# Output operands of an adaptive-layernorm block prepared in two steps, the layernorm written in place, the output pools laid out in another order, and the slices of down weights taken earlier

## The chip, the cores and the metric

The kernel runs on one core of a Trainium2 chip. The metric is the device time of one execution in microseconds (us); lower is better. Differences of less than about 0.3% can't be told from no change.

## The reference

Everything is float32. There are two sequences (b = 0, 1) of 1024 tokens of 1024 features. A vector per sequence gives six modulation vectors (shift, scale and gate for the attention and for the feed-forward part).

```python
mod = (_silu(L0_c) @ L0_wmod).reshape(L0_c.shape[0], 6, 1, -1)
...
h = _layernorm(x, axis=-1) * (1 + ca) + sa
x = x + ga * _L0_attn_ref(h, ...)     # 32 heads of 32, q/k layernorm, ALiBi, causal softmax, output projection
h = _layernorm(x, axis=-1) * (1 + cb) + sb
x = x + gb * _L0_ffn_ref(h, ...)      # out = (silu(gate) * up) @ Wd.T * ad, inner width 2752
```

## The kernel before

All large products are done by a Strassen-like scheme with seven products of half-size blocks (`seven`, names P1, P2, U2, P5, U3, P53, U6 in this order), which needs sums of blocks of both operands (S1 to S4 of the left one, T1 to T4 of the weights). The kernel has these stages:

1. Projections to q, k and v of sequence 0, then of sequence 1 (`projections`), in pairs of token tiles: a pair j is 256 tokens, four pairs per sequence and per part q, k, v. In the loop over the pairs of sequence 1 the function `side` is called after each of the seven products. It advances `down_weights`, which forms the sums T1 to T4 of the feed-forward part's down weights in 20 slices: each slice loads four blocks of 128 KB, subtracts four times on GpSimd (lines 1215 to 1218) and stores four blocks (line 1221), in three steps, 60 steps in all. In the kernel before, the first step comes at call 24 of 84.
2. Attention (`attention`), in units of one group of four heads and one block of keys: scores on TensorE, exponentials on ScalarE (line 1085), masks on GpSimd (line 1089), the product with v on TensorE, and sums of the probabilities on VectorE and GpSimd (line 1117). At the end of a group `settle` adds up the sums with a product with ones, and for the last group of 512 queries `reciprocals` marks these queries as settled.
3. Output projection, residual and second layernorm (`output`), pair by pair: four pairs of sequence 0, then two of sequence 1 beside the attention of sequence 1, then the last two of sequence 1 beside other feed-forward rows (`rest_rows`).
4. The feed-forward part: gate and up products, then down products.

`together` interleaves stage 2 with stages 1 and 3: it takes units of attention and pieces of dense work by a share of their planned times, so TensorE's instructions follow an order written at build time, in which they are pinned. The order of the other engines' instructions, and of the loads and stores that SyncE issues, is made by the framework's scheduler, which simulates the program and takes whatever is ready by its own estimate, earlier program lines first. It is therefore not the program order, but it is fixed at build time, and each engine then works through its own list in order.

What one output pair does: `operand` makes the left operand. It loads the reciprocals of the softmax sums (rb, four loads, line 1249) and four blocks of the attention's output (aoA: A11, A12, A22, A21, line 1263), multiplies each block by the reciprocals (line 1264, two on VectorE and two on GpSimd), and forms S1, S2 on VectorE and S3, S4 on GpSimd (lines 1265 to 1269; S3 overwrites A21). Of its tiles only A21 has two buffers; rb, A11, A12, A22, S1, S2, S4 have one. `output` then loads the residual (xr, two tiles of 128 x 1024, line 1292), runs the seven products, and `read` evacuates each: P1, U2 and P5 are copied by ScalarE (line 1299), the others are added on VectorE (1307, or 1305 for U6), multiplied by the gate ga and added to xr on GpSimd (1308, 1309). The sum xr is stored to x1 (line 1314) and normalized into a second tile xn (`normalize`: statistics at 729 and 730, reciprocal root at 734 to 745, the result at 747). In the pair after, xn is transposed by TensorE in four pieces through the one shared bank, which VectorE empties into h2t (line 869); h2t is stored for the feed-forward part (lines 1200, 1329). The shared bank also serves `settle` (the matmul with ones, emptied at 1127).

Memory: pools are stacked in the order in which they are opened, and a pool's first use waits until every earlier pool that it overlaps has been released. The output stage's pools (hb, wo, oga, tok, opart, osmall, ao, restw) take the place of the projections' pools (a, w, raw, part, qs, xin, qsmall) and of the slices' pool (wdsum) above them. The first pair's operand is made ahead of the output weights (wB_o and wT_o, lines 824 and 828). restw holds the last columns of the gate and up weights (line 1374, 1.5 MB).

Of the kernel before, what the change touches and what calls it, by code (L numbers as in the profile page):

```python
# [12 lines left out]
FP = mybir.dt.float32  # L13
# [5 lines left out]
P = 128  # L19
# [461 lines left out]
def kernel(  # L481
# [20 lines left out]
    B, S, D = x.shape  # L502
# [6 lines left out]
    QB = 512  # L509
# [41 lines left out]
    NJ = NT // 2  # L551
# [111 lines left out]
    with tc.tile_pool(name="prep", bufs=1) as prep, tc.tile_pool(  # L663
        name="wmod", bufs=2 * KC
# [176 lines left out]
    def seven(a, bt, banks, read, between, grain):  # L841

        x, y = banks.pair()
        for c_, qa, qb_, q in SEVEN:
            bank = x if c_ == "x" else y
            first = q in ("P1", "P2", "P5")
            for j in range(KC // 2):
                matmul(
                    bank, a(qa, j), bt[qb_][:, j, :],
                    start=(first and j == 0), stop=(j == KC // 2 - 1), skip_group_check=True,  # L850
                )
                if j % grain == grain - 1 and j < KC // 2 - 1:
                    banks.made += 1
                    yield grain * MM
                    yield from between(q)
            read(q, bank)
            banks.made += 1
            yield grain * MM
            yield from between(q)
# [154 lines left out]
    settled = set()  # L1014
# [169 lines left out]
    def alone(dense):  # L1184
        for _ in dense:
            pass
# [56 lines left out]

    def operand(b, j, ap_, own=None):

        qb, y0 = 2 * j * P // QB, 2 * j * P % QB
        rb = ap_.tile([P, KC, 2 * P], FP, tag="rb", name=f"rb_{b}_{j}")
        for g in range(4):
            nc.sync.dma_start(
                rb[ts(g, HD)],  # L1250
                rec_dram[b][qb].rearrange("(k g) q -> g k q", g=4)[g][:, ds(y0, 2 * P)].partition_broadcast(HD),
            )
        a = {
            q: (ap_ if q == "S4" or own is None else own).tile(
                [P, KC // 2, P], FP, tag=q, name=f"ao{q}_{b}_{j}",
                bufs=2 if q == "A21" and own is None else None,
            )
            for q in ("A11", "A12", "A21", "A22", "S1", "S2", "S4")
        }
        for m, kh, q, eng in (  # L1260
            (0, 0, "A11", nc.vector), (0, 1, "A12", nc.gpsimd), (1, 1, "A22", nc.vector), (1, 0, "A21", nc.gpsimd),
        ):
            nc.sync.dma_start(a[q], ao_dram[b][qb][:, ds(kh * 4, 4), ds(y0 + m * P, P)])
            eng.tensor_mul(a[q], a[q], rb[:, ds(kh * 4, 4), ts(m, P)])
        nc.vector.tensor_add(a["S1"], a["A21"], a["A22"])
        nc.vector.tensor_sub(a["S2"], a["S1"], a["A11"])  # L1266
        a["S3"] = a["A21"]
        nc.gpsimd.tensor_sub(a["S3"], a["A11"], a["A21"])
        nc.gpsimd.tensor_sub(a["S4"], a["A12"], a["S2"])
        return a  # L1270

    gates = {}

    def output(b, js, pools, banks, bt, todo, keep, made={}, q0=1):

        gap_, ap_, tkp, partp, hbp, sm = pools
        while (b, 2 * js[0] * P // QB) not in settled:
            yield None
        if b not in gates:
            gates[b] = gap_.tile([P, D], FP, tag="ga", name=f"ga_{b}")  # L1280
            nc.sync.dma_start(gates[b], gate_dram[2][b].partition_broadcast(P))
        ga = gates[b]

        for j in js:
            while (b, 2 * j * P // QB) not in settled:
                yield None
            qts = (2 * j, 2 * j + 1)
            a = made.get((b, j)) or operand(b, j, ap_)
            xs = []
            for m in range(2):  # L1290
                xr = tkp.tile([P, D], FP, tag="xr", name=f"xr_{b}_{qts[m]}")
                nc.sync.dma_start(xr, x[b, ts(qts[m], P), :])
                xs.append(xr)
            part_t = {}

            def read(q, bank):
                if q in ("P1", "U2", "P5"):
                    part_t[q] = partp.tile([P, 512], FP, tag=q, name=f"o{q}_{b}_{j}")
                    nc.scalar.copy(part_t[q], bank)
                    return  # L1300
                m, n = QUAD[q]

                yg = part_t[MATE.get(q, "P5")]
                if q == "U6":
                    nc.vector.tensor_mul(yg, ga[:, ts(n, HALF)], bank)
                else:
                    nc.vector.tensor_add(yg, yg, bank)
                    nc.gpsimd.tensor_mul(yg, yg, ga[:, ts(n, HALF)])
                nc.gpsimd.tensor_add(xs[m][:, ts(n, HALF)], xs[m][:, ts(n, HALF)], yg)

            yield from seven(lambda q, i: a[q][:, i, :], bt, banks, read, todo.places(q0, 1), 2)
            yield from todo.run(len(todo.list), True)
            for m in range(2):
                nc.sync.dma_start(x1_dram[b * NT + qts[m]], xs[m])
            xn = []
            for m in range(2):
                t_ = tkp.tile([P, D], FP, tag="xn", name=f"xn_{b}_{qts[m]}", bufs=2)
                xn.append(t_)
            todo.first(normalize(xs, xn, sm, f"f{b}_{j}"), b == 1 and j >= NJ // 2 - 1)
            h2 = keep(b, j)  # L1320
            for m in range(2):
                for g in range(2):
                    def go(bank, m=m, g=g, xn=xn, h2=h2, j=j):
                        turned(
                            xn[m], bank, lambda k: h2[:, k, m, :],
                            lambda k: modt[:, 4, k, b : b + 1], lambda k: modt[:, 3, k, b : b + 1], g, False,
                        )
                        if (m, g) == (1, 1):
                            nc.sync.dma_start(h2_dram[b][j], h2)
                            if b == 0:  # L1330
                                inner_b("B11", h2[:, 0 : KC // 2], j, hbp, nc.vector)
                                inner_b("B21", h2[:, KC // 2 :], j, hbp, nc.vector)
                    todo.add(go)
# [21 lines left out]
    OUT_US = 112.0  # L1355
# [70 lines left out]
    with ExitStack() as st:  # L1426
# [9 lines left out]
        banks = Banks(three[0:2], three[2:3] + more[2:5])  # L1436
# [52 lines left out]
    ost = ctx.enter_context(ExitStack())  # L1489
# [8 lines left out]
    out_args = []  # L1498

    def dense_work():  # L1500
        yield from dense0
        with tc.tile_pool(name="wdsum", bufs=2) as dwp:
            steps = itertools.chain.from_iterable(down_weights(i, dwp) for i in range(4 * NSB))

            def side(n, e):

                if 7 * n + e >= 24:
                    next(steps, None)

            yield from projections(1, qpools, banks, 1, side=side)  # L1510
            for _ in steps:
                pass
        early.close()
        hbp = right["hb"] = ost.enter_context(tc.tile_pool(name="hb", bufs=1))
        wop = ost.enter_context(tc.tile_pool(name="wo", bufs=1))
        gap_, tkp, partp, osm, aop = [
            ost.enter_context(tc.tile_pool(name=n, bufs=k))
            for n, k in (("oga", 1), ("tok", 3), ("opart", 1), ("osmall", 1), ("ao", 1))
        ]
        opools = (gap_, aop, tkp, partp, hbp, osm)  # L1520
        made = {(0, 0): operand(0, 0, opools[1])}
        bt = weights_b(wop, wout_t, "o", wt_dram[3])
        rwp = ost.enter_context(tc.tile_pool(name="restw", bufs=1))
        out_args.extend((opools, banks, bt, Todo(banks), keep))
        yield from output(0, range(NJ), *out_args, made)
        right["w"] = rest_weights(rwp, nc.sync)
        yield from output(1, range(NJ // 2), *out_args)

# [13 lines left out]
    opools, _, bt, todo, _ = out_args  # L1542
# [3 lines left out]
    wide = rest_st.enter_context(tc.tile_pool(name="wide", bufs=1, side="right"))  # L1546
# [20 lines left out]
    fetch(0, 0, nc.scalar)  # L1567
    rest_w = right["w"]
    fetch(1, 0, nc.scalar)
    made = {(1, NJ // 2): operand(1, NJ // 2, opools[1], wide)}  # L1570
    made[1, NJ // 2 + 1] = operand(1, NJ // 2 + 1, opools[1])
    fetch(0, 1)
    with_turns(rows((0, 0), (1, 0)))
    fetch(1, 1)
# [1 line left out]
    def between():  # L1576
        yield from rows((0, 1))
        second(0)
        yield from rows((1, 1))

    together(
        between(), output(1, range(NJ // 2, NJ), *out_args, made, 3), lambda a: 0.6 * OUT_US / 2 * a / 20.6
    )
    in_range(rest_pool, rps)
    fetch(0, 2)
# [53 lines left out]
    with ExitStack() as ff:  # L1639
# [9 lines left out]
        with ExitStack() as gu:  # L1649
# [83 lines left out]
            for s in range(NSB):  # L1733
# [66 lines left out]
                for n_, (oa, ob, frm, to) in enumerate(STAGES):  # L1800
# [18 lines left out]
                    for e, (c_, qa, qb_, q) in enumerate(CHAIN):  # L1819
                        bt = bts[e] if e < len(bts) else moving(s, n_, e)  # L1820
                        for mat in ("g", "u"):
# [7 lines left out]
                            f_, t_ = tiles[mat]  # L1829
# [222 lines left out]
```

## Time and profile before

| quantity | value |
|---|---|
| median of three timed runs | 2902.21 us (2901.19 to 2909.03) |
| profiled execution: its time, its span | 2896.01 us, 2894.3 us |
| TensorE matmul busy | 2702.2 us (93%) |
| VectorE, ScalarE, GpSimd busy | 1453.0, 685.2, 1296.8 us |
| moved by DMA | 579.14 MB, mean 200 GB/s |
| HBM read, written | 411.89 MB, 165.17 MB |
| first and last matmul with output weights | 916.0, 1495.6 us |

Times within the kernel count from the start of the profiled span. PE is TensorE, PEld its weight loads, DVE VectorE, ACT ScalarE, POOL GpSimd, and SPq SyncE's queue, which issues the loads and stores. A wait is put down to what ended last before it; where a row waits for several things, the one named need not be the one that mattered. A busy share is a mean over a stretch and doesn't say who waits for whom.

### The profile page before, as it was taken

What the parts mean: (1) busy time and instruction counts of PE and PEld (TensorE: products, weight loads), DVE (VectorE), ACT (ScalarE), POOL (GpSimd) and SP (SyncE); (2) the same over time, 40 slices, a digit from 0 to 9 for tenths busy, and PEclk for the clock granted to TensorE, in tenths of its full rate; (3) what the DMA queues carried; (4) which work ended last, traced back from release to release, by engine and by line L of the source; (5) the groups of instructions that cost most, each with busy time, mean ns of one, the idle gap of its engine ahead of it and who ended that gap; (6) DMA issues with size and microseconds to landing.
All of it is one profiled execution on the core that took longest, in us unless ns stands there. A gap on an engine that the chain in (4) does not pass through costs nothing.

```text
span 2894.3 us, 29930 instructions
## 1 busy us (share of the span) xinstructions
PE 2702.2 (93%) x10271; PEld 1330.2 (46%) x10271; DVE 1453.0 (50%) x2285; ACT 685.2 (24%) x1523; POOL 1296.8 (45%) x1270
## 2 busy tenths in 40 slices
PE   6999999999997787878989999999999998999998
PEld 2444433333332222222655444444444446888776
DVE  5766535665543356665554453454535346444442
ACT  1322244444443555545110011010101100000000
POOL 3312033345655565556457364464735541222342
PEclk9999999999998899999999999999999999999999
DMA  9878763756557444342687667585766659555542
GB/s 342 311 270 311 284 219 117 236 181 220 191 164 236 130 153 134 124 124 77 208 262 241 211 225 235 169 285 160 268 190 206 229 169 286 158 146 146 158 144 81
DMA packets 377573, 579.14 MB, mean 200 GB/s; under 512 B 21590, under 2 KB 278712, under 8 KB 366276
## 3 DMA queue, kind: packets, MB, share of 16 engines
q1 hardware_dynamic: 363928, 556.12, 59.2%
q10 hardware_dynamic: 13484, 21.02, 2.2%
q8 instruction: 84, 1.38, 0.2%
q14 instruction: 77, 0.63, 0.1%
HBM read 411.89 MB, written 165.17 MB: 199 GB/s over the span
## 4 chain that ended last, share of the span: by engine, by line
PE 43%; DMA 4%; DVE 3%; issue 3%; POOL 3%; ACT 1%; SPq 0%; POOLq 0%; DVEq 0%; ACTq 0%
PE gx L1824 7%; PE ux L1824 7%; PE dx L1949 7%; PE gy L1824 6%; PE uy L1824 6%; PE dy L1949 5%; PE bank L763 1%; DMA bt<-bop_B 1%; DMA bop_T<-inner_T 1%; PE sc L763 1%; ACT p L1085 1%; DMA wuA<-in_L_ffn_Wu_dram 1%; PE rest L763 0%; PE av L763 0%; DVE asS L1778 0%
## 5 line engine op out<-in xcount | busy, mean ns | idle before, releaser
L1085 ACT ACTIVATE p<-sc,kw 128x128 f32<-128x128 f32 (+3 forms) x1024 | 421.6, 513 | 394.9 <-PE sc L763 376.7
L763 PE MATMUL bank<-wT,a 128*128 128x512 f32 x768 | 353.6, 603 | 12.0 <-DVE wT L832 6.8
L1117 POOL TENSOR_TENSOR p<-p,p 128x1024 f32<-128x1024 f32 (+3 forms) x128 | 262.1, 2048 | 183.4 <-PE av L763 157.5
L1117 DVE TENSOR_TENSOR p<-p,p 128x1024 f32<-128x1024 f32 (+3 forms) x192 | 246.2, 1291 | 153.4 <-POOL p L1089 97.3
L763 PE MATMUL bank<-wB,a 128*128 128x512 f32 x576 | 262.5, 601 | 1.2 <-DVE raw L982 0.6
L763 PE MATMUL sc<-cq,ck 32*128 32x512 f32 (+3 forms) x1536 | 194.5, 548 | 56.4 <-ACT p L1085 56.1
L1089 POOL TENSOR_SCALAR_AFFINE_SELECT p<-p 128x256 f32<-128x256 f32 x256 | 139.3, 556 | 200.8 <-ACT p L1085 194.7
L763 PEld LDWEIGHTS bank<-wT,a 128*128 128x128 f32 x768 | 140.0, 192 | 186.2 <-issue 168.9
L763 PE MATMUL av<-p,cv 128*32 128x512 f32 (+3 forms) x1536 | 173.2, 514 | 17.2 <-POOL p L1089 17.2
L763 PEld LDWEIGHTS bank<-wB,a 128*128 128x128 f32 x576 | 104.5, 190 | 145.0 <-issue 123.6
L763 PEld LDWEIGHTS sc<-cq,ck 32*128 32x128 f32 x1536 | 64.5, 186 | 193.6 <-ACT p L1085 103.0
L1824 PE MATMUL gy<-bt,sig 128*128 128x512 f32 x280 | 132.4, 595 | 10.7 <-DMA bt<-bop_B 5.7
L1824 PE MATMUL uy<-bt,siu 128*128 128x512 f32 x280 | 131.6, 592 | 0.0
L1824 PE MATMUL gx<-bt,sig 128*128 128x512 f32 x280 | 131.6, 592 | 0.0
L1824 PE MATMUL ux<-bt,siu 128*128 128x512 f32 x280 | 131.6, 592 | 0.0
L763 PEld LDWEIGHTS av<-p,cv 128*32 128x32 f32 x1536 | 34.0, 110 | 138.7 <-issue 80.7
L1824 PEld LDWEIGHTS gy<-bt,sig 128*128 128x128 f32 x280 | 52.4, 190 | 80.8 <-issue 71.1
L763 PE MATMUL bank<-wB_o,aoA 128*128 128x512 f32 x128 | 68.3, 667 | 18.7 <-DVE aoS L1266 17.7
L1824 PEld LDWEIGHTS uy<-bt,siu 128*128 128x128 f32 x280 | 53.2, 190 | 67.0 <-issue 65.8
L1824 PEld LDWEIGHTS ux<-bt,siu 128*128 128x128 f32 x280 | 53.2, 190 | 67.0 <-issue 65.5
L1824 PEld LDWEIGHTS gx<-bt,sig 128*128 128x128 f32 x280 | 53.2, 190 | 67.0 <-issue 65.7
L1824 PE MATMUL ux<-bt,wuS 128*128 128x512 f32 x160 | 75.2, 592 | 0.0
(415 smaller groups left out, 4467.9 us busy)
## 6 DMA issues: line engine op xcount, KB each, us to landing
bt<-bop_T SPq DMA_DIRECT2D x140, 512.0 KB
bt<-bop_B SPq DMA_DIRECT2D x99, 512.0 KB
a<-hop SPq DMA_DIRECT2D x20, 1792.0 KB
wm<-in_L_wmod_dram SPq DMA_DIRECT2D x48, 512.0 KB
wB<-in_L_attn_Wqkv_dram SPq DMA_DIRECT2D x21, 1024.0 KB
aq_S<-act_S SPq DMA_DIRECT2D x16, 1280.0 KB
qk<-qs SPq DMA_DIRECT2D x16, 1024.0 KB
act_S<-asS SPq DMA_DIRECT2D x30, 512.0 KB
```

Of the source, the lines that this page charges most:

```text
L763: return in_order(nc.tensor.matmul(*args, **kw_))
L1085: last_exp[0] = nc.scalar.activation(p[:, g, lo:hi], sp[:, g, lo:hi], AF.Exp, bias=kw[:, d, h_ : h_ + 1])
L1089: last_mask[0] = nc.gpsimd.affine_select(out=p[:, :, 0:P], in_=p[:, :, 0:P], pattern=[[0, 2], [1, P]], compare_op=ALU.is_ge, fill=0.0, bas ...
L1117: adders[b](half, jb).tensor_add(dst, dst, ps[half][:, :, 0:n])
L1824: nc.tensor.matmul(ps.rearrange("p (j t) -> p j t", j=NJ), ins[mat][qa][:, c2, :], bt[:, :, c2, :], start=(q in ("P1", "P2", "P5") and c2 ...
L1949: nc.tensor.matmul(bank[c_], ins[qa][:, s, :], wt[qb_][:, s, :], start=(q in ("P1", "P2", "P5") and s == 0), stop=(s == NSB - 1), skip_gro ...
```

## The change

`operand` becomes a generator with two steps: the first allocates the tiles and issues all eight loads, the second multiplies and forms the sums. A22 gets a second buffer, as A21 has. While a pair's products run, `ahead` takes the first step for the next pair at the third product (U2) and the second step at the seventh (U6), if the attention of the next pair's queries is settled by then; other pairs are made in one go (`operands`). The layernorm's result is written over the residual sum (`xn = xs`) instead of into tiles of its own, and the pool tok has four xr tiles instead of three xr and two xn tiles. The pool restw is opened ahead of ao instead of after it, so it lies below ao. The slices of down weights start at call 12 of `side` instead of call 24.

```diff
     def operand(b, j, ap_, own=None):
...
-                bufs=2 if q == "A21" and own is None else None,
+                bufs=2 if q in ("A21", "A22") and own is None else None,
...
-        for m, kh, q, eng in (
+        blocks = (
             (0, 0, "A11", nc.vector), (0, 1, "A12", nc.gpsimd), (1, 1, "A22", nc.vector), (1, 0, "A21", nc.gpsimd),
-        ):
+        )
+        for m, kh, q, eng in blocks:
             nc.sync.dma_start(a[q], ao_dram[b][qb][:, ds(kh * 4, 4), ds(y0 + m * P, P)])
+        yield
+        for m, kh, q, eng in blocks:
             eng.tensor_mul(a[q], a[q], rb[:, ds(kh * 4, 4), ts(m, P)])
         nc.vector.tensor_add(a["S1"], a["A21"], a["A22"])
         nc.vector.tensor_sub(a["S2"], a["S1"], a["A11"])
         a["S3"] = a["A21"]
         nc.gpsimd.tensor_sub(a["S3"], a["A11"], a["A21"])
         nc.gpsimd.tensor_sub(a["S4"], a["A12"], a["S2"])
-        return a
+        made[b, j] = a
+        yield
+
+    def operands(b, j, *args):
+        alone(operand(b, j, *args))
+        return made[b, j]
+
+    made = {}
...
-            a = made.get((b, j)) or operand(b, j, ap_)
+            a = made.get((b, j)) or operands(b, j, ap_)
...
+            step = {}
+            nxt = (b, j + 1) if j + 1 < NJ else (b + 1, 0)
+
+            def ahead(e):
+                if e == 2 and nxt not in made and not step and (nxt[0], 2 * nxt[1] * P // QB) in settled:
+                    step[0] = operand(*nxt, ap_)
+                    next(step[0])
+                elif e == 6 and step and nxt not in made:
+                    next(step[0])
...
-            yield from seven(lambda q, i: a[q][:, i, :], bt, banks, read, todo.places(q0, 1), 2)
+            yield from seven(lambda q, i: a[q][:, i, :], bt, banks, read, todo.places(q0, 1, ahead), 2)
...
-            xn = []
-            for m in range(2):
-                t_ = tkp.tile([P, D], FP, tag="xn", name=f"xn_{b}_{qts[m]}", bufs=2)
-                xn.append(t_)
+            xn = xs
             todo.first(normalize(xs, xn, sm, f"f{b}_{j}"), b == 1 and j >= NJ // 2 - 1)
...
-                if 7 * n + e >= 24:
+                if 7 * n + e >= 12:
                     next(steps, None)
...
-        gap_, tkp, partp, osm, aop = [
+        gap_, tkp, partp, osm, rwp, aop = [
             ost.enter_context(tc.tile_pool(name=n, bufs=k))
-            for n, k in (("oga", 1), ("tok", 3), ("opart", 1), ("osmall", 1), ("ao", 1))
+            for n, k in (("oga", 1), ("tok", 4), ("opart", 1), ("osmall", 1), ("restw", 1), ("ao", 1))
         ]
         opools = (gap_, aop, tkp, partp, hbp, osm)
-        made = {(0, 0): operand(0, 0, opools[1])}
+        operands(0, 0, opools[1])
         bt = weights_b(wop, wout_t, "o", wt_dram[3])
-        rwp = ost.enter_context(tc.tile_pool(name="restw", bufs=1))
...
-    made = {(1, NJ // 2): operand(1, NJ // 2, opools[1], wide)}
-    made[1, NJ // 2 + 1] = operand(1, NJ // 2 + 1, opools[1])
+    operands(1, NJ // 2, opools[1], wide)
+    operands(1, NJ // 2 + 1, opools[1])
```

More of the change, by code (lines that the diff above doesn't have):

```diff
@@ L1269, in operand, with output @@
         nc.gpsimd.tensor_sub(a["S4"], a["A12"], a["S2"])
-        return a
+        made[b, j] = a
[4 more added lines that the diff above has]
+    made = {}
     gates = {}
-    def output(b, js, pools, banks, bt, todo, keep, made={}, q0=1):
+    def output(b, js, pools, banks, bt, todo, keep, q0=1):
         gap_, ap_, tkp, partp, hbp, sm = pools
@@ L1515, in dense_work @@
         wop = ost.enter_context(tc.tile_pool(name="wo", bufs=1))
-        gap_, tkp, partp, osm, aop = [
+        gap_, tkp, partp, osm, rwp, aop = [
             ost.enter_context(tc.tile_pool(name=n, bufs=k))
-            for n, k in (("oga", 1), ("tok", 3), ("opart", 1), ("osmall", 1), ("ao", 1))
+            for n, k in (("oga", 1), ("tok", 4), ("opart", 1), ("osmall", 1), ("restw", 1), ("ao", 1))
         ]
         opools = (gap_, aop, tkp, partp, hbp, osm)
-        made = {(0, 0): operand(0, 0, opools[1])}
+        operands(0, 0, opools[1])
         bt = weights_b(wop, wout_t, "o", wt_dram[3])
-        rwp = ost.enter_context(tc.tile_pool(name="restw", bufs=1))
         out_args.extend((opools, banks, bt, Todo(banks), keep))
-        yield from output(0, range(NJ), *out_args, made)
+        yield from output(0, range(NJ), *out_args)
         right["w"] = rest_weights(rwp, nc.sync)
@@ L1581 @@
     together(
-        between(), output(1, range(NJ // 2, NJ), *out_args, made, 3), lambda a: 0.6 * OUT_US / 2 * a / 20.6
+        between(), output(1, range(NJ // 2, NJ), *out_args, 3), lambda a: 0.6 * OUT_US / 2 * a / 20.6
     )
```

## The prediction

> **What bounds the kernel now.** The page first: TensorE (PE) is busy 93% of the span, so only time in which PE stands still can be won, and only where the change reaches it. The change touches the output stage (about 880 to 1510 us) and the slices of down weights before it (536 to 887 us).
>
> ```profile
> PE 2702.2 (93%) x10271; PEld 1330.2 (46%) x10271; DVE 1453.0 (50%) x2285; ACT 685.2 (24%) x1523; POOL 1296.8 (45%) x1270
> ```
>
> Then the windows of 20 us (columns: window, length, PE, PEld, DVE, ACT, POOL busy, granted PE clock, DMA share, GB/s). Before 900 PE is full; from 900 to 920 it does 4 us of work at DMA share 0.98.
>
> ```profile
> 880.00:900.00 20.00, 18.29 (x97) 6.32 (x96) 4.51 (x7) 9.46 (x18) 8.03 (x12) 1.00 0.79 193
> 900.00:920.00 20.00, 4.02 (x8) 1.33 (x12) 3.29 (x4) 0.00 (x0) 5.78 (x4) 0.57 0.98 323
> ```
>
> The waits of PE from 898 to 1400 tell who ends them (total us, times, longest). ACT's exponentials (47 us) and masks are attention's own; the change can reach the second row, one wait of 17.7 us, and the fourth, two waits of 15.2 us together.
>
> ```profile
> PE sc L763 <- ACT p L1085: 46.8, 41, 3.7
> PE bank L763 <- DVE aoS L1266: 17.7, 1, 17.7
> PE av L763 <- POOL p L1089: 17.2, 7, 5.1
> PE bank L763 <- DVE h2t L869: 15.2, 2, 8.6
> ```
>
> The timeline around the first wait (start, length, engine, line, operation, idle time before it):
>
> ```profile
> 888.92 0.37 SPq L1374 DMA_DIRECT2D restw<-in_L_ffn_Wg_dram  x1
> 892.91 1.35 SPq L1249 DMA_DIRECT2D rb<-rec  x1
> 897.22 1.06 PE L763 MATMUL bank<-p,ones 128*32 128x512 f32 x8
> 901.07 5.78 SPq L1263 DMA_DIRECT2D aoA<-ao  x4
> 906.95 3.68 SPq L824 DMA_DIRECT2D wB_o<-in_L_attn_Wout_dram  x2
> 915.98 3.67 PE L763 MATMUL bank<-wB_o,aoA 128*128 128x512 f32 x4 [17.70 <-DVE aoS L1266]
> ```
>
> The output weights can go out once the last projection matmul is over (896), but SyncE reaches them at 906.95, behind the restw, rb and ao loads. By the trace's semaphore records SyncE's loads use eight semaphores in turn, and here each issue follows the landing of the load eight before it (899.90 after 899.88, 901.07 after 901.05): the queue is full. The first weight block lands at 915.58, PE starts at 915.98. So the weights end this wait; the VectorE row named had only just ended too.
>
> The two 15.2 us waits have one pattern. Lines of the first, then of the second:
>
> ```profile
> 998.84 0.33 SPq L1292 DMA_DIRECT2D xr<-_attn_hidden_states_dram  x1
> 1001.23 0.45 SPq L1263 DMA_DIRECT2D aoA<-ao  x1
> 1011.02 0.71 DVE L1264 TENSOR_TENSOR aoA<-aoA,rb 128x512 f32<-128x512 f32 x1 [10.95 <-DMA aoA<-ao]
> 1013.06 1.94 PE L763 MATMUL bank<-p,ones 128*32 128x512 f32 x8 [6.65 <-DVE h2t L869]
> ...
> 1085.93 0.35 SPq L1292 DMA_DIRECT2D xr<-_attn_hidden_states_dram  x1
> 1087.01 0.64 SPq L1249 DMA_DIRECT2D rb<-rec  x1
> 1094.59 1.27 POOL L1264 TENSOR_TENSOR aoA<-aoA,rb 128x512 f32<-128x512 f32 x1 [10.15 <-DMA rb<-rec]
> 1105.82 1.94 PE L763 MATMUL bank<-p,ones 128*32 128x512 f32 x8 [8.59 <-DVE h2t L869]
> ```
>
> A residual load xr waits until the layernorm of the pair before (L747) has read its buffer; the operand loads stand behind it on SyncE and leave late, in a burst; their multiplications already stand in the queues of VectorE and GpSimd, ahead of the evacuation h2t that frees PE's shared bank. SyncE's own waits (880 to 1400) price the cause:
>
> ```profile
> SPq L1263 <- PE bank L763: 32.6, 13, 8.0
> SPq L1292 <- DVE xn L747: 31.0, 5, 9.4
> ```
>
> **What the Trainium skill says.** "Perfetto Trace Analysis", section on the Tensor Engine instruction: ACT, DVE and GpSimd are strict FIFO. The trace agrees: VectorE is idle 10.95 us with evacuations behind L1264. "TensorE: Matmul & The Clock Gate", Part 1: after an idle window of about 3.4 us the array runs at half clock for about as long. It agrees: four matmuls took 3.67 us after the 17.7 us wait, 1.98 elsewhere. "GPSIMD Engine Reference", 3.1: a two-input elementwise operation is about twice as slow there; here L1264 takes 1266 ns on POOL, 702 on DVE. "DMA: Bandwidth & Descriptors", Latency: the fixed cost grows with load; here a 512 KB store lands in 2.6 us when quiet, 6.5 us when crowded.
>
> **Part 1: pools in another order, slices sooner, first operand early (gain 13).** A pool waits for all pools whose memory it overlaps. By the shapes, per partition: projections' a 0-28 KB, w 28-84, raw 84-100, part 100-106, qs 106-114, xin 114-122, small to 123, wdsum 123-133. Before, ao lies at 102-126 and waits for part (free at 892) and wdsum (last store landed 888.9). After, tok shrinks from 20 to 16 KB, restw (12) goes ahead of ao, and ao lies at 110-136: over nothing that the value projection uses. Wdsum remains. Its 60 steps ran from 536 to 887, 5.95 us each; 12 steps sooner is 71 us, so it is free near 816 to 835. The first operand (8 loads, 2 MB, and 8 elementwise operations) then runs some 60 us ahead of its use. restw (1.5 MB) now waits for raw and goes behind the output weights. So at 896 SyncE is free for the first weight block. Its landing: issue 896.5, then between 4 us (2.6 us for a quiet 512 KB, plus another 512 KB at 1.4; the next weight blocks landed 2.7 us per MB apart) and 8.6 us (what it took at 906.95), that is 900.5 to 905.1. I take 903: gain 915.98 - 903 = 13, bounds 11 and 15.5. The slow clock after the wait (3.67 - 1.98 = 1.7 us) I leave as it is, since about 5 us of wait remain; gain bound 1.7.
> What it costs: the operand's elementwise work, 2 x 0.70 + 2 x 0.69 = 2.8 us on VectorE and 4 x 1.27 = 5.1 on GpSimd, leaves an idle slot and lies beside the value projection, where PE is 98% busy and needs both for evacuations and masks. Cover: GpSimd is 60% busy there and loses the slices' work (4 x 0.72 us in each 18). Cost 1, bounds 0 and 4. The slices' 160 DMAs of 128 KB and 80 subtractions move from late to early pairs, past SyncE's hop and attention loads and behind masks on GpSimd; GpSimd is 40% busy at 450 to 550. Cost 0, bounds -1 and 2. restw's 1.5 MB x 2.7 = 4 us of DMA come into the crowded stretch after the weights, 2 MB (5.4 us) leave it: 0.
>
> **Part 2: operands in two steps, second A22, layernorm in place, four xr (gain 9).** No PE work changes, nor its order. The queues of the others are not in program order already (the second pair's rb loads leave at 920.82, inside the first pair), so the two steps shift priorities, not whole blocks. What truly changes: A22 has two buffers, so it needn't wait for the last product of the pair before (part of L1263's 32.6 us), and xr has four, so its load needn't wait for L747 (31.0 us). With that the cause of the 6.65 and 8.59 us waits goes; next late are the exponentials, whose waits stay. I take 60% of 15.2, 9 us; bounds 0 and 22 (also two mask waits of 3.75 and 3.42 us at 1235 and 1267, where L1268 and L1264 stand ahead of masks on GpSimd).
> The added wait: L747 now overwrites what the store to x1 (L1314) reads, so it waits for that landing, with attention's adds and evacuations behind it on VectorE. From issue of the second store to L747 there are 12.3, 9.8, 14.0, 8.7, 14.8, 2.3, 4.2 and 6.7 us over the eight pairs; the stores land in 2.6 to 6.5. Only the sixth (store landed 1401.18, L747 at 1400.19) is short, by 1 us. Cost 1, bounds 0 and 5; without the cover of the slow statistics chain it would be 8 x 3 = 24 us on VectorE.
>
> **Sum.** 13 + 9 - 1 - 1 = 20 us. Against the profiled execution (2896.01, span 2894.3) that gives 2876; that run is 6.2 us below the median of 2902.21, against which I state it: 2882. The later stages start sooner by the same, as PE is nearly full from 1550 on.
>
> **Rivals.**
> Start only: another entry on SyncE (h2t stores wait 49.5 us, x1 stores 47.0) takes xr's place ahead of the operand loads, and part 2 gives nothing: 2902.2 - 13 + 2 = 2891. For it: SyncE waits for many things; against: both bad cases show xr just ahead.
> The start is DMA-bound anyway: value stores and the attention chunk hold the weights until 905 and the missing ga and xr hold the first residuals: 5 - 2 = 3, 2899. Against: the weights came at 2.7 us per MB, faster than PE used them.
> Slower: the multiplications, now with priority over the last product's evacuation and residual sum, stand in the FIFO queues ahead of loads that haven't landed at all five handovers under attention, not at two: 5 x 7.6 - 15.2 = +23, less 13, plus 2: 2914. It decides from the point where the loads leave SyncE later than the multiplications' place: the two steps are four products apart, a pair takes 69 us (916 to 985), so some 40 us, against landings of 3 to 10 us and a longest SyncE wait of 13.9. That speaks against it; that the queue order comes from a planner's estimate speaks for it.
>
> **Chances.** Forecast 0.54 (own range 2866 to 2893), start only 0.20, DMA-bound 0.11, slower 0.15. About 0.3% (8.7 us) can be told from no change: faster below 2893.5. Faster 0.53 + 0.13 + 0.01 = 0.67, same 0.17, slower 0.16. The range 2866 to 2905 leaves out the slower rival and the joint upper bounds.
>
> **What would show it.** PE's wait at the first output product falls to about 5 us; the first operand's loads stand near 820 to 840; restw follows wB_o; L1292 no longer waits for L747; the h2t waits go. Wrong if the first operand is still issued after 890, if L747 waits several us for a store, or if L1264 idles longer than 25 us in total on DMA.

## The result and the profile after

| | median, us | lowest to highest | profiled execution, its span |
|---|---|---|---|
| before | 2902.38 (4 runs) | 2901.19 to 2909.03 | 2896.01, 2894.3 |
| after | 2859.35 (4 runs) | 2851.89 to 2861.48 | 2851.89, 2850.2 |

The ratio after to before is 0.9835, 95% interval 0.9818 to 0.9853: 43.0 us faster by the medians. The forecast was 2882 with a range of 2866 to 2905, so the direction was right and the time fell outside the range: the gain is about twice the forecast of 20.

TensorE's own work is what it was; the first line of the page:

```profile
PE 2698.4 (95%) x10271; PEld 1329.8 (47%) x10271; DVE 1454.4 (51%) x2285; ACT 685.5 (24%) x1523; POOL 1292.9 (45%) x1270
```

The windows of 20 us that answer to those of before. PE, which did 4.02 us of work from 900 to 920, now does 16.01, and before 900 the DMA share is 0.17 where it was 0.79:

```profile
880.00:900.00 20.00, 20.00 (x102) 7.40 (x102) 4.66 (x7) 8.71 (x19) 8.17 (x10) 1.00 0.17 53
900.00:920.00 20.00, 16.01 (x65) 4.58 (x64) 8.16 (x5) 5.87 (x12) 7.68 (x4) 0.83 0.93 353
```

The waits of PE from 898 to 1360 (total us, times, longest). The exponentials stay (46.8 before). The 17.7 us wait is 4.0, the mask waits (17.2 before) are 4.0, and the two waits for h2t (15.2 before) are one of 4.5:

```profile
PE sc L763 <- ACT p L1085: 45.6, 42, 3.8
PE bank L763 <- DVE h2t L869: 4.5, 1, 4.5
PE bank L763 <- issue: 4.0, 1, 4.0
PE av L763 <- POOL p L1089: 4.0, 4, 2.1
```

The timeline around the first output product. The first operand's loads leave at 839 and 844, and restw's first load leaves 25 us after the first output weights instead of 18 us ahead of them:

```profile
839.31 1.81 SPq L1250 DMA_DIRECT2D rb<-rec  x4
843.83 7.67 SPq L1265 DMA_DIRECT2D aoA<-ao  x6
...
901.54 0.38 SPq L824 DMA_DIRECT2D wB_o<-in_L_attn_Wout_dram  x1
907.57 3.75 PE L763 MATMUL bank<-wB_o,aoA 128*128 128x512 f32 x4 [3.99 <-issue]
926.44 0.43 SPq L1393 DMA_DIRECT2D restw<-in_L_ffn_Wg_dram  x1
```

**Where the time came from.** PE's matmuls stand in the same order in every kernel here, so each can be compared with itself: the time of a matmul before, less its time after, is what has been gained up to there. At 895 us of before's profile the profile after is 5.3 us late. Between 895 and 917, where the output products begin, it gains 13.7. From 917 to 1345, the output products of sequence 0 under attention, it gains 34.3. From there to the end it gains 1.5. Together 44.2, and the spans differ by 44.1.

The 5.3 us ahead of 895 are not the change. The other twelve profiled executions are 0.3 to 8.6 us late there as well, whether their slices start at call 12 (0.3 to 8.6) or 24 (3.8 to 7.9): the one profile of before that the prediction worked with was an early one. The trace shows where the 5.3 arise. By 100 us the profile after is 1.2 us early; it then loses 3.1 us between 100 and 165, 1.7 at 298 and 1.7 at 486, and at each of these places its granted clock is at half for 3.4 us (0.76 as a mean from 153 to 160, where before has 1.00).

The sums of the busy-time windows over the stretch from 917 to 1345, first before, then after (the same 1968 matmuls; columns as above):

```profile
916.50:1345.00 428.50, 351.06 (x1968) 112.94 (x1966) 236.00 (x324) 220.78 (x541) 257.06 (x234) 0.92 0.45 141
```

```profile
908.10:1302.30 394.20, 343.91 (x1968) 110.46 (x1966) 230.89 (x321) 220.92 (x541) 248.94 (x229) 0.94 0.51 157
```

Of the 34.3 us, 7.2 are the same matmuls at a better clock (351.06 to 343.91; by the trace's clock record 64.4 us of this stretch are at half clock before, 45.3 after), and 27.1 are idle time. By the waits of PE in this stretch these are: masks 17.2 to 4.0, that is 13.2; h2t 15.2 to 4.5 and 0.9, that is 9.8; the layernorm's result 2.8 to 0; exponentials 41.9 to 40.7, that is 1.2. That makes 27.0.

### The profile page after: what moved, and what is told of

It is laid out like the page before. It is cut to its first block, busy times and chain, and to the rows that moved or that the text cites. A ratio compares the mean times of both kernels' runs of the same rounds, so it can differ in the third digit from the quotient of the medians.

```text
span 2850.2 us, 29927 instructions
## 1 busy us (share of the span) xinstructions
PE 2698.4 (95%) x10271; PEld 1329.8 (47%) x10271; DVE 1454.4 (51%) x2285; ACT 685.5 (24%) x1523; POOL 1292.9 (45%) x1270
## 5 line engine op out<-in xcount | busy, mean ns | idle before, releaser
L763 PE MATMUL bank<-wT,a 128*128 128x512 f32 x768 | 359.9, 613 | 12.0 <-DVE wT L832 6.8
L1842 PE MATMUL gy<-bt,sig 128*128 128x512 f32 x280 | 132.5, 596 | 10.9 <-DMA bt<-bop_B 6.0
L1842 PE MATMUL gx<-bt,wgS 128*128 128x512 f32 x160 | 75.2, 592 | 0.0
```

Of the source, the lines that this page charges most:

```text
L763: return in_order(nc.tensor.matmul(*args, **kw_))
L1842: nc.tensor.matmul(ps.rearrange("p (j t) -> p j t", j=NJ), ins[mat][qa][:, c2, :], bt[:, :, c2, :], start=(q in ("P1", "P2", "P5") and c2 ...
```

## Experiments

"First" is the gain between 895 and 917 of before's time, "stage" that from 917 to 1345, both from the one profile of each kernel, matmul by matmul. A handover is the passage from one pair of the output stage to the next.

| kernel | first | stage | median, us | ratio to before, 95% interval |
|---|---|---|---|---|
| after | 13.7 | 34.3 | 2859.35 | 0.9835 (0.9818 to 0.9853) |
| e1: pools and slices alone | 8.8 | 0.4 | 2895.37 | 0.9971 (0.9961 to 0.9981) |
| e7: e1, restw over raw | 13.5 | -1.2 | 2888.38 | 0.9949 (0.9935 to 0.9963) |
| e8: after, slices at 24 | 7.6 | 33.7 | 2864.68 | 0.9867 (0.9847 to 0.9887) |
| e2: all but pools and slices | -2.4 | 34.5 | 2875.23 | 0.9908 (0.9888 to 0.9928) |
| e3: in place with four xr, alone | -2.4 | 11.8 | 2889.72 | 0.9947 (0.9928 to 0.9966) |
| e4: two steps alone | 0.4 | -1.7 | 2901.8 | 1.0003 (0.9991 to 1.0015) |
| e5: in place, four xr, second A22 | -2.9 | 29.8 | 2880.42 | 0.99 (0.9868 to 0.9931) |
| e6: in place, four xr, two steps | -2.9 | 12.2 | 2891.38 | 0.9953 (0.9934 to 0.9971) |
| e10: after without the two steps | 13.7 | 34.1 | 2853.31 | 0.9829 (0.9806 to 0.9853) |
| e13: after with one A22 | 14.1 | 12.9 | 2871.49 | 0.9897 (0.9869 to 0.9925) |
| e11: after, second A11 | 13.6 | 30.7 | 2858.9 | 0.9844 (0.9819 to 0.987) |
| e12: after, second A12 | 13.8 | 36.5 | 2854.58 | 0.983 (0.9806 to 0.9854) |

The columns leave out what an execution gains or loses ahead of 895 and after 1345. After 1345 the kernel after gains 1.5, but e2 loses 6.1, e3 5.7 and e5 9.0. Of that 3.8, 3.9 and 4.8 us are lost between 2200 and 2600 us, in the feed-forward part, where the three have 13.6 or 13.7 us at half clock and before has 6.8. The profiled execution is also one draw: that of the kernel after was its fastest of four, those of e3, e5, e6 and e12 their slowest (in e3 2900.2 with a median of 2889.72).

### The two parts alone

The theory at this point was that the parts add up; the rival, that one opens the way for the other.

```diff
 e1, against before (tok stays as it was)
-            for n, k in (("oga", 1), ("tok", 3), ("opart", 1), ("osmall", 1), ("ao", 1))
+            for n, k in (("oga", 1), ("tok", 3), ("opart", 1), ("osmall", 1), ("restw", 1), ("ao", 1))
-                if 7 * n + e >= 24:
+                if 7 * n + e >= 12:
 e2, against after: these two lines as they were before, tok with four xr
```

> The kernel before with part 1 alone: restw opened ahead of ao, slices of down weights from call 12; the operand, xr and xn as before. Additive theory (the two parts don't need one another): 13 us faster, 2889, ratio 0.9955, PE's wait ahead of the first output product about 4 us. Theory that the parts interact (the gain of the handovers needs the new pools too): 13 us plus some of the 35 us that the output stage under attention gained, 2880 or less.

> The changed kernel without part 1: pools in the order of before, slices from call 24; two-step operand, second A22, four xr and layernorm in place stay. Additive theory: the first wait stays at 17 us and the output stage under attention gains 35 us, 2867, ratio 0.988. Interaction: 2875 or more.

By the medians e1 gains 8.0 us (2903.32 to 2895.37) and e2 28.1 (2903.32 to 2875.23), together 36 against 43.0. So the part that was forecast as the smaller is by far the larger. Neither theory holds as it was written: e1's gain is short of both (its first wait is 8.9 us, not 4), and e2's time is at the edge of the rival's range (2875), though its stage gains 34.5 as the additive theory had it. The missing 7 us lie within the spread of the medians, but 4.9 of them can be seen in the first step of the profiles: 8.8 in e1 against 13.7. (By itself part 2 loses 2.4 there.) The timeline of e1 shows why:

```profile
900.58 0.38 SPq L1374 DMA_DIRECT2D restw<-in_L_ffn_Wg_dram  x1
...
908.57 0.40 SPq L824 DMA_DIRECT2D wB_o<-in_L_attn_Wout_dram  x1
915.75 3.70 PE L763 MATMUL bank<-wB_o,aoA 128*128 128x512 f32 x4 [8.86 <-DMA wB_o<-in_L_attn_Wout_dram]
```

The restw loads leave ahead of the output weights. In e1 tok still has 20 KB a partition, which puts restw at 102 to 114 KB, above raw (84 to 100). There it overlaps part (100 to 106) and qs (106 to 114) alone, and its first load waits 9.5 us for VectorE's line 984, which reads part. In the kernel after, tok has 16 KB, restw lies at 98 to 110 over the top of raw as well, and must wait for the value stores. So the place in the list of pools was not enough; the address should do it, and the address came from the other part of the change.

### restw put over raw

```diff
 e7, against e1
-        gap_, tkp, partp, osm, rwp, aop = [
+        gap_, tkp, rwp, partp, osm, aop = [
-            for n, k in (("oga", 1), ("tok", 3), ("opart", 1), ("osmall", 1), ("restw", 1), ("ao", 1))
+            for n, k in (("oga", 1), ("tok", 3), ("restw", 1), ("opart", 1), ("osmall", 1), ("ao", 1))
```

> As e1 (pools and slices alone), but restw opened ahead of opart, so that it lies over raw and its loads have to wait for the value stores. Theory that in e1 restw's loads ahead of the weights cost the missing 5 us: restw leaves SyncE after wB_o, PE's first wait falls from 8.9 to about 4 us, 5 us faster than e1, 2890. Theory that the output weights are late for another reason (the value stores themselves): the wait stays at 8 to 9 us, 2895.

Gain 16.3 us by the medians (2904.65 to 2888.38), first step 13.5. The output weights now come first, and PE's wait there is 4.2 us, as in the kernel after (4.0):

```profile
899.36 0.38 SPq L824 DMA_DIRECT2D wB_o<-in_L_attn_Wout_dram  x1
...
921.74 2.14 SPq L1374 DMA_DIRECT2D restw<-in_L_ffn_Wg_dram  x1
```

So the address was the cause of the lost 5 us: with restw over raw the order of the loads, the wait and the first step are those of the kernel after. With e7's 16.3 in the place of e1's 8.0 the parts add up within the spread: 16.3 + 28.1 = 44.4 against 43.0.

### The slices of down weights

```diff
 e8, against after
-                if 7 * n + e >= 12:
+                if 7 * n + e >= 24:
```

> The changed kernel with the slices of down weights from call 24 again. Theory that the early operand needs wdsum's early release: the first operand's loads leave after 887 and stand ahead of wB_o, the first wait is back at 12 to 17 us, 2868 to 2872, 10 us or so slower than the changed kernel. Theory that the pools' order alone gives it: as the changed kernel, 2859.

```profile
892.69 1.32 SPq L1250 DMA_DIRECT2D rb<-rec  x3
...
904.67 1.83 SPq L824 DMA_DIRECT2D wB_o<-in_L_attn_Wout_dram  x2
912.14 3.75 PE L763 MATMUL bank<-wB_o,aoA 128*128 128x512 f32 x4 [10.10 <-DVE aoS L1270]
```

About half of what was expected is lost: 6.1 us of the first step (13.7 to 7.6). The first operand waits for wdsum again (rb at 892.69, not 839.31), so its loads stand ahead of the weights, but restw no longer does. The earlier slices are worth 6.1 us on top of the pools' order. The order alone, with part 2 in place, takes the first step from -2.4 (e2) to 7.6 (e8); what of these 10.0 us is restw's place and what is ao's was not separated.

### Which edit of part 2

```diff
 e3, against before
-            for n, k in (("oga", 1), ("tok", 3), ("opart", 1), ("osmall", 1), ("ao", 1))
+            for n, k in (("oga", 1), ("tok", 4), ("opart", 1), ("osmall", 1), ("ao", 1))
-            xn = []
-            for m in range(2):
-                t_ = tkp.tile([P, D], FP, tag="xn", name=f"xn_{b}_{qts[m]}", bufs=2)
-                xn.append(t_)
+            xn = xs
 e4, against before: operand, operands and ahead as after, with
+                bufs=2 if q == "A21" and own is None else None,
 e5, against e2
-            yield from seven(lambda q, i: a[q][:, i, :], bt, banks, read, todo.places(q0, 1, ahead), 2)
+            yield from seven(lambda q, i: a[q][:, i, :], bt, banks, read, todo.places(q0, 1), 2)
 e6, against e2
-                bufs=2 if q in ("A21", "A22") and own is None else None,
+                bufs=2 if q == "A21" and own is None else None,
```

The theories were that the layernorm in place does it (SyncE is no longer held by the xr load), that the second A22 does, or that the two steps do (the operand's place in the planner's order).

> The kernel before with the layernorm in place and four xr tiles alone. Theory SyncE block (xr's load waiting for the layernorm holds the operand loads behind it): at least 25 us faster, 2877 or less. Theory A22 (its single buffer keeps the sums at the start of their own pair, ahead of masks): 10 us faster or less, 2892 to 2900. Theory planner's place (the two steps give the work an earlier place): the same as A22's here.

> The kernel before with the operand in two steps during the pair ahead alone; A22 has one buffer, xn its own tiles, xr three. Theory planner's place: 20 us faster, 2882. Theories SyncE block and A22: within 5 us of before, since the loads still wait for the same buffers and xr still stands ahead of them.

> As e2 (in place, four xr, second A22, pools and slices of before), but the operand made in one go at its own pair, not in steps during the pair ahead. Theory A22 (the planner takes what is ready, so a free buffer is all that the early work needs): as e2, 2875, ratio to before 0.991. Theory place (the two steps are needed as well, since the planner takes earlier program lines first): 2885 to 2890, near e3.

> As e2, but A22 with one buffer: in place, four xr and the two steps. Theory A22: as e3, 2890, ratio 0.995, with the mask waits of 4.0 and 5.2 us at the handovers still there. Theory place: as e2, 2875.

Waits of PE from 895 to 1400, first in e4, then in e3, then in e5:

```profile
PE av L763 <- POOL p L1089: 15.8, 7, 5.1
PE bank L763 <- DVE h2t L869: 14.7, 2, 7.6
```

```profile
PE av L763 <- POOL p L1089: 11.9, 5, 5.1
PE bank L763 <- DVE h2t L869: 6.2, 2, 5.5
```

```profile
PE bank L763 <- DVE h2t L869: 4.5, 1, 4.5
PE av L763 <- POOL p L1089: 4.0, 4, 2.1
```

The two steps alone leave both rows nearly as they were (15.2 and 17.2 before), and SyncE's residual loads, line 1303 in that kernel, still wait for the layernorm to read its tile:

```profile
SPq L1303 <- DVE xn L747: 30.9, 5, 9.5
```

So the theory of the planner's place falls. The layernorm in place with four xr takes the h2t row from 15.2 to 6.2, as the prediction had reasoned, and the stage gains 11.8. By the medians e3 is 13.6 us faster: less than the 25 of the first theory, more than the 10 that the second allowed. The mask row falls only from 17.2 to 11.9; the second A22 takes it to 4.0. In the stage e5 gains 29.8; e6, which has the steps instead, gains 12.2, and its two rows are those of e3 (11.9 and 6.1). e5's median lies between the times named for the two theories; its ratio of 0.99 covers the 0.991 of the A22 theory, and its waits decide for it. What in place and what the fourth xr tile do was not separated, since without a tile for xn the xr tiles live longer. A second A22 without the layernorm in place was not measured; that A22 needs the other edit is therefore not shown.

### Taking one edit out of the whole

```diff
 e10, against after
-            yield from seven(lambda q, i: a[q][:, i, :], bt, banks, read, todo.places(q0, 1, ahead), 2)
+            yield from seven(lambda q, i: a[q][:, i, :], bt, banks, read, todo.places(q0, 1), 2)
 e13, against after
-                bufs=2 if q in ("A21", "A22") and own is None else None,
+                bufs=2 if q == "A21" and own is None else None,
```

> The changed kernel whole, except that operands are made in one go and not in two steps ahead. Theory: the steps count only on top of the second A22 and the layernorm in place, by what the part-2 kernels differed with and without them (step of 33.0 against 28.3 us): 4 to 5 us slower than the changed kernel, about 2864, and the A22 chains near 1239 and 1338 stay as they are. Rival (the steps do nothing anywhere, the 5 us were chance of the two builds): 2859.

> The changed kernel whole, except that A22 has one buffer again. Theory (the second A22 and the layernorm in place work only together): it loses the two handovers near 1239 and 1338 and the mask waits of GpSimd behind A22's multiplication return to 8 to 12 us; 16 to 20 us slower than the changed kernel, 2875 to 2879. Rival (with the pools in the new order, the first operand made early and tok smaller, A22 no longer matters): 2859 to 2863.

The two steps are worth nothing in the changed kernel: the stage gains 34.1 without them and 34.3 with them, and the intervals of the ratios cover each other. The traces show why. Read instruction by instruction, VectorE, GpSimd, TensorE and SyncE work through the same list in both kernels, as far as operation, tile name, shape and line tell; ScalarE's differs by one swap of neighbours, at 1463 us. The framework's scheduler gave the work the same places with and without the two steps. The two medians are 6.0 us apart all the same, which is a measure of what such a difference between two runs is worth.

The theory of 4 to 5 us falls too. In e2 and e5 the lists differ in eleven places, all between 943 and 964 us; the 4.7 us between them arise later, between 1200 and 1300 of before's time, most of them in steps of 0.4 to 0.5 us a matmul where the clock of e5 is at half and that of e2 is not. A stage value can thus move by some 5 us with the clock alone.

The second A22 holds. Without it the stage gains 12.9 instead of 34.1, and e13 is 18.2 us slower than e10, which ran on the same chip (16 to 20 were expected against the kernel after). Its waits of PE from 895 to 1360 are those of e3:

```profile
PE av L763 <- POOL p L1089: 11.8, 5, 5.1
PE bank L763 <- DVE h2t L869: 6.2, 2, 5.5
```

The timeline of e13 shows one such wait whole (lines picked from 1202 to 1220; 1269 and 1272 form S1 and S3 of the operand, 1089 is the mask):

```profile
1202.80 0.37 SPq L1265 DMA_DIRECT2D aoA<-ao  x1
...
1210.71 0.64 DVE L1268 TENSOR_TENSOR aoA<-aoA,rb 128x512 f32<-128x512 f32 x1
...
1211.38 0.69 DVE L1269 TENSOR_TENSOR aoS<-aoA,aoA 128x512 f32<-128x512 f32 x1
...
1212.15 1.64 POOL L1272 TENSOR_TENSOR aoA<-aoA,aoA 128x512 f32<-128x512 f32 x1 [1.98 <-DVE aoS L1269]
...
1213.76 0.85 POOL L1089 TENSOR_SCALAR_AFFINE_SELECT p<-p 128x256 f32<-128x256 f32 x1
...
1214.66 1.07 PE L763 MATMUL av<-p,cv 128*32 128x256 f32 x4 [3.73 <-POOL p L1089]
1215.66 3.78 PE L763 MATMUL bank<-wB_o,aoA 128*128 128x512 f32 x4
```

A load of the operand leaves late, at the end of the pair before. Its multiplication and S1 on VectorE come when the next pair begins, GpSimd stands 1.98 us in front of S3, and the mask that PE needs is queued behind S3. PE waits 3.73 us, and its next four matmuls take 3.78 us. In the kernel after, the sums of this operand were begun at 1171.9, 37 us ahead of the handover. GpSimd stood idle in front of its S3 there too, for 4.95 us, but no mask that PE needed was behind it. At the handover the same matmuls come with the masks done first:

```profile
1208.60 1.96 POOL L1089 TENSOR_SCALAR_AFFINE_SELECT p<-p 128x256 f32<-128x256 f32 x4
...
1209.06 0.98 PE L763 MATMUL av<-p,cv 128*32 128x256 f32 x8 [0.92 <-POOL p L1089]
...
1209.97 1.55 PE L763 MATMUL bank<-wB_o,aoA 128*128 128x512 f32 x3
```

That one place is a step of 4.0 us between the two kernels; the next handover of this kind is one of 5.1. Over the stretch the 1968 matmuls are busy 354.99 us in e13 and 344.07 in e10: half of the 21 us that A22 is worth are matmuls at a slower clock (68.3 us of the stretch are at half clock in e13, 45.5 in e10), not waits.

### A second buffer for one more block

```diff
 e11, against after (e12 the same with "A12")
-                bufs=2 if q in ("A21", "A22") and own is None else None,
+                bufs=2 if q in ("A21", "A22", "A11") and own is None else None,
```

> The changed kernel with a second buffer for A11 as well (2 KB). Theory: after the change what is left in this stage are the exponentials, 45.6 us, and no other wait above 4.5; so nothing is won, 2856 to 2862. Rival (the operand loads' 36.5 us of waiting on SyncE for the last product still delay loads that others need): 2851 to 2855.

> The changed kernel with a second buffer for A12 (2 KB), which GpSimd multiplies. Theory: the exponentials bound this stage, nothing is won, 2856 to 2862. Rival (A12 is GpSimd's, so its late load holds masks as A22's did): 2851 to 2855, with the mask wait of 4.0 us gone.

Neither can be told from the kernel after by its ratio. With A11 doubled the mask waits are 6.5 us in place of 4.0 and the stage gains 30.7. With A12 doubled, the block that GpSimd multiplies, the mask wait falls from 4.0 to 2.3 us and the stage gains 36.5 against 34.3; both differences are within what the clock alone moves. The time of e12, 2854.58, lies in the range of its rival (2851 to 2855), but e10, which has the queues of the kernel after and ran on the same chip, took 2853.31, so nothing was won:

```profile
PE sc L763 <- ACT p L1085: 45.6, 42, 3.8
...
PE av L763 <- POOL p L1089: 2.3, 4, 0.9
```

Nothing was won, as the theory had it, and the exponentials' 45.6 us are by far the largest row that is left. That they bound the stage now was not tested. No version here is shown to beat the kernel after; e10 does the same with less program.

## Why the prediction was wrong

**Part 1, gain 13 (11 to 15.5): right.** The first step is 13.7. The first operand left at 839.31 (forecast: memory free at 816 to 835), restw left after the weights, and PE started 6.0 us after the first weight load was issued (forecast 903 - 896.5 = 6.5). The prediction's addresses already had the smaller tok, but its sum took the 13 for part 1 by itself; e1 and e7 show that 5 of the 13.7 us hang on tok being smaller, which is part 2's doing.

**Cost of the operand beside the value projection, 1 us: nothing seen.** PE is busy 20.00 us of the 20 from 880, and between 840 and 895 the profile after neither gains nor loses a tenth of a microsecond. The earlier slices cost nothing that stands out of the scatter ahead of 895.

**Part 2: this failed, at the step "I take 60% of 15.2, 9 us; bounds 0 and 22".** The mechanism of the h2t waits was right, and they gave 9.8, not far from the 9 taken (the 60% had no derivation, so that nearness is luck). But they are less than a third of what the stage gained. The other terms of the 34.3 were left out of the sum: masks 13.2, the better clock 7.2, the layernorm's result 2.8, exponentials 1.2. The mask row, 17.2 us in seven waits, stood in the prediction's own list as attention's own. Two of the seven (3.75 and 3.42) were seen to come from the operand's S3 and one of its multiplications on GpSimd and were put into the upper bound alone; with the clock they were never priced at all. The sum rests on the prediction's first sentence, that only time in which PE stands still can be won, and the 7.2 us of clock show that this is not so. That clock was named: by the Trainium skill, "TensorE: Matmul & The Clock Gate", Part 1, the array runs at half clock after an idle window of about 3.4 us. It was then used for one wait of the first step, as a bound of 1.7 us, and not for the waits of part 2, though the long ones have it as well (3.78 us for four matmuls after a wait of 3.73 in e13). The runs show half clock beside shorter waits too: in before's profile it begins at 1001.4 and lasts 3.4 us, and the only wait just ahead is one of 1.7 us.

**The second A22** was named as one of two true changes, but as help for SyncE's queue. It did little there: the operand loads' waits for a product (PE's tiles of the name bank) are 32.6 us before and 36.5 after (first line below, SyncE from 880 to 1400), and 39.8 in e13, which lacks the buffer. What the buffer does is to let one multiplication, and the four sums behind it, come before the handover and not in front of the next pair's masks; that is worth 21 us once the layernorm is in place. The residual loads' 31.0 us behind the layernorm did go; they now wait 17.5 us for transposes:

```profile
SPq L1265 <- PE bank L763: 36.5, 17, 5.4
SPq L1303 <- PE bank L766: 17.5, 7, 6.8
```

**The added wait, 1 us: right in place, short in size.** Only one layernorm waits for a store of x1, as forecast, but 3.9 us instead of 1, which the prediction itself had named as a sign of being wrong, and PE waits 3.2 us for it (the step in the comparison is -3.4, at 1403 of before's time). By the landings in the trace the first of the two stores left at 1351.26 and landed at 1360.17, and the layernorm followed at 1360.27. So this landing took 8.9 us, longer than any of the 2.6 to 6.5 us that the prediction had. Its price of 1 us came from before's profile, where the same store took 6.2 us (1394.99 to 1401.18); the 2.7 us more are nearly all of what the price was short. VectorE's row from 880 to 1480:

```profile
DVE xr L747 <- DMA x<-xr: 3.9, 1, 3.9
```

**The rivals.** "Start only" falls: part 2 gives 28 us by itself (e2). "DMA-bound anyway" falls: the first wait is 4.0. "Slower" falls: GpSimd's multiplications idle 7.0 and 4.1 us on the loads of rb and A and VectorE's 1.3, from 880 to 1480, not 38 (GpSimd's 2.9 more on a store); and the two steps, whose priority was to cause it, do nothing.

**The sum again.** 13.7 + 34.3 + 1.5 - 5.3 = 44.2 between the profiles. The 5.3 are chance, of which the prediction had taken account by moving from its profile (2896.01) to the median (2902.21).

## What to carry to other kernels

When a change takes a late operation out of a queue, price everything that stands behind it in that queue, on each engine, by the whole row of waits and not by the two examples that were looked at; and add to each wait of PE the slower matmuls that follow it. When a buffer is doubled, ask which operation it lets come earlier and what that operation stood in front of, not only whose load it frees. When pools are put in another order, work out the addresses: which pool waits for which follows from overlap, and another pool's size can decide it.

## What had not been expected of the hardware and the profile

- The clock took as much as a row of waits: 7.2 us of the stage's 34.3, and 10.9 (354.99 - 344.07) of the 21 us between e13 and e10, on the same 1968 matmuls. In e3, where the waits had fallen, the same matmuls took 355.83 us, more than the 351.06 before. Its clock record has 70.1 us of that stretch at half clock, that of before 64.4. Equal waits don't bring equal stretches: one wait of 3.75 us for exponentials early in the stage has 6.8 us of half clock beside it in before (from 953.6) and 10.2 in e3 (from 962.7). What decides that is open.
- Executions differ by up to 9 us ahead of 895 us, and by up to 7.7 us already at 300 us, where the code is the same in all of them. A single profile compared with another by its span alone would carry this as a gain or a loss; compared matmul by matmul it is seen and set aside.
- An edit of the program's order may change nothing: the two steps left the lists of TensorE, VectorE, GpSimd and SyncE as they were. The lists are worth comparing before a reason for a gain is sought.
